# Classes by one comparison, keys read with a step, and the last layer's mask on ScalarE for four tiles at once

## The chip, the cores and the metric

The kernel runs on one core of one Trainium2 chip. A core has five engines with queues of their own: TensorE (PE in the profile, its weight loads PEld), VectorE (DVE), ScalarE (ACT), GpSimd (POOL) and SyncE (SP), which only starts DMAs. They work in parallel and wait for one another by semaphores; SBUF is the memory that all of them use, PSUM the one that TensorE writes its products to. The metric is the device time of one execution in microseconds. A kernel is timed in several runs, of which the median counts; one more execution is recorded by the hardware profiler.

## The reference, cut to what matters

The input is 16 graphs (batches) of 1024 nodes with 64 channels, and a dense, sparse-valued matrix `adj` of 1024 x 1024 for each. Layer 0 averages over neighbours; layer 1 takes quantiles over a thinned list of neighbours and passes them through two small matrix products:

```python
h = relu(layernorm(x))
x = x + (adj / clip(adj.sum(2), 1)) @ h           # layer 0
h = relu(layernorm(x))
# layer 1, for every node i of a graph:
nb      = (adj with ones on the diagonal, > 0), without i itself
m       = number of nb
skip    = (m + 1) // 2 if m > 10 and mask else 1
removed = every skip-th of nb, if skip > 1;  also removed from the other end
vals    = h[j] for all j still linked to i, i itself among them
agg     = 0.25*quantile(vals, .25) + 0.5*quantile(vals, .5) + 0.25*quantile(vals, .75)
y       = (relu((h + agg) @ W1 + b1) @ W2 + b2) * mask[i]
x       = x + y
```

The quantiles are taken per channel, so a node with m neighbours needs 64 columns of up to m + 1 values sorted. In these inputs an average node has few neighbours and a few nodes have very many.

## The kernel before, in words

**Tiles.** The 1024 nodes of a batch are 8 tiles of 128 rows. The batches are taken in four groups of four (`GROUPS`). Work on a batch is written as generators ("streams"), among them `loads`, `signs`, `transposes`, `products`, `channels`, `listing` and `endings`:

- `signs` and `listing` make, for each row of `adj`, the keys of its neighbours: ScalarE takes the sign (and sums it into `total`), VectorE multiplies by a falling column number (`sg<-sg,keyed`) and takes the eight largest of each of four segments (MAX8 into `rec`).
- `transposes` and `products` are layer 0: TensorE transposes `adj` into PSUM (`pt`), ScalarE copies to `att`, TensorE multiplies into `ps_small`, VectorE divides by the degree and adds `x` (`row<-ps_small,deg`).
- `channels` normalises and writes a table of rows (`tab`) to device memory.
- `endings` (line 772) sorts a batch's nodes by the length of their list. It makes a class number `d` for each node (lines 788 to 800) and from it `hot`, a one-hot array of 23 classes x 8 tiles. TensorE sums `hot` over nodes into a `ps_small` buffer `pc`; VectorE makes from it each node's place (`base`, `pos`, `to`); GpSimd scatters the rows to their places in `srt[g]`, one indirect DMA per tile.

When all four batches of a group have ended, `group(g)` (line 1294) reads back the sorted rows (`recs`), fetches one row of `adj` per partition for the nodes with most neighbours (`gat_rows<-in_adj_dram,hnodes_i`), corrects the table by a scatter (`tab<-drop,didx`), makes indices, and starts a `Job` (line 870) for each class of list length. The 32 nodes of each batch with the longest lists, 512 in all and four per partition, go to `long_lists` (line 1433), which takes them in four passes: each gathers one row of `adj` per partition (`gat_rows<-in_adj_dram,lnodes_i`) and makes the keys from it (`lkey`), since these lists are too long for `rec`.

**Jobs.** A group's sorted nodes are 31 tiles in ten length classes, of 1 to 6 tiles. A job gathers the lists from the table: one indirect DMA of GpSimd for each place of a list and tile (`places<-tab,idx`; `lplaces<-whole,lidx` for long lists). VectorE marks removed places (`rem`), sorts by a network of minima and maxima (`places`, `other`), and weighs the quantile places (`w`, `prod`). `layers` (line 1156) is the last step: for every chunk of up to four tiles TensorE sums and transposes the weighed rows (`pt`), ScalarE copies them (`ot`), TensorE multiplies by W1 (`ph`, a `ps_small` buffer), ScalarE applies the bias and the maximum (`hid`), TensorE multiplies by W2 (`py`, a `ps_small` buffer), and VectorE makes `y`, the masked product plus the residual. GpSimd scatters `y` to the output.

**What sets the order.** The tiles in PSUM come from small pools; `ps_small` has three buffers, shared by `products`, `endings`, `layers` and others. Each stream says at its yields on which engine it goes on and from when. A planner (`Plan`, line 246) keeps a modelled clock for every engine, and always runs the stream that can begin first, ties going by rank. The instructions are written to the engines' queues in that order, and for VectorE and GpSimd that order is kept (`manual_schedule`, line 377). So a due time is a position in a queue, not a wait. The constants that shift due times are `SLACK` (2.0), `LOOSE` (7.0) and `LATE` (14.0), in the planner's microseconds:

```python
yield "DVE", lambda: at(py) + LATE          # layers: y is due 14 after py
yield "PE", lambda: max(at(hid) + SLACK, room("ps_small", 3))
yield "POOL", lambda: at(y) + LATE          # the scatter of y
```

All instructions that the planner books pass through one helper at line 240, so the profile shows line 240 for nearly everything, and the groups are told apart by the names of their tiles.

Of the kernel before, what the change touches and what calls it, by code (L numbers as in the profile page):

```python
# [9 lines left out]
F32 = mybir.dt.float32  # L10
BF = mybir.dt.bfloat16
HF = mybir.dt.float16
I32 = mybir.dt.int32
U8 = mybir.dt.uint8
AF = mybir.ActivationFunctionType
OP = mybir.AluOpType
AX = mybir.AxisListType

P = 128
# [4 lines left out]
HUGE = 1.0e30  # L24
# [2 lines left out]

GROUPS = (4, 4, 4, 4)
NSEG = 4
STEPS = (16, 19, 22, 29, 39, 59, 79)  # L30
CLS = 15 + len(STEPS) + 1

# [10 lines left out]
LSEG = 8  # L45
# [181 lines left out]
SLACK = 2.0  # L227
LOOSE = 7.0
LATE = 14.0
# [16 lines left out]
class Plan:  # L246
# [33 lines left out]
    def at(self, *tiles):  # L280
        return max(self.ready.get(t.tensor.name, INF) for t in tiles)
# [104 lines left out]
def list_path(ctx, tc, x, adj, nodemask, w1, b1, w2, b2, out, go):  # L386
    nc = tc.nc
    B, N, C = x.shape
    H = w1.shape[1]
    CO = w2.shape[1]  # L390
    NT = N // P
# [15 lines left out]
    consts = ctx.enter_context(tc.tile_pool(name="consts", bufs=1))  # L407
    dram = ctx.enter_context(tc.tile_pool(name="dram", bufs=1, space=bass.MemoryType.DRAM))
    grp = ctx.enter_context(tc.tile_pool(name="grp", bufs=2))
# [22 lines left out]
    col_f = consts.tile([P, N], F32, name="col_f")  # L432
# [5 lines left out]
    nc.vector.memset(zero_f, 0.0)  # L438
    place1 = consts.tile([P, P], F32, name="place1")
    nc.vector.tensor_scalar(place1, col[:, :P], 1.0, None, op0=OP.add)  # L440
    cls_i = grp.tile([P, N], I32, name="gat_rows", bufs=1)[:, :CLS * NT]
    cls_i = cls_i.rearrange("p (c t) -> p c t", t=NT)
    nc.gpsimd.iota(cls_i, pattern=[[-1, CLS], [0, NT]], base=CLS - 1, channel_multiplier=0)
    cls = consts.tile([P, CLS, NT], F32, name="cls")
    nc.vector.tensor_copy(cls, cls_i)
    row_i = consts.tile([P, NT], I32, name="row_i")
    nc.gpsimd.iota(row_i, pattern=[[P, NT]], base=0, channel_multiplier=1)
    row_f = consts.tile([P, NT], F32, name="row_f")
# [323 lines left out]
    def endings(pool, now):  # L772

        first = lambda rank: rank - 3000
        for b, st in enumerate(batch):
            now[0] = b
            g = max(g for g in range(NG) if FIRST[g] <= b)
            size = GROUPS[g]
            yield "ACT", lambda: known(st, "rec", "row") if st["listed"] == NT else INF
            rec, total, row = st["rec"], st["total"], st["row"]  # L780

            for t in range(NT):
                nc.scalar.activation(
                    row[:, t, R0:R0 + 8 * NSEG], rec[:, t, :], AF.Relu, bias=before[:, t:t + 1]
                )


            yield "DVE", always
            found = new(pool, [P, NT, 8 * NSEG], BF, "found", 1)
            nc.vector.tensor_scalar(found, rec, 0.0, None, op0=OP.is_gt)  # L790
            d = new(tiny, [P, NT], F32, "d", 2)
            nc.vector.tensor_reduce(d, found, AX.X, OP.add)
            full = new(tiny, [P, NT], F32, "full", 2)
            nc.vector.tensor_reduce(
                full, found.rearrange("p t (s e) -> p t s e", e=8)[:, :, :, 7], AX.X, OP.max
            )
            nc.vector.scalar_tensor_tensor(d, full, float(STEPS[0]), d, op0=OP.mult, op1=OP.max)
            nc.vector.tensor_scalar(d, d, float(STEPS[0]), None, op0=OP.min)
            for s in STEPS[1:]:
                nc.vector.scalar_tensor_tensor(d, total, float(s), d, op0=OP.is_gt, op1=OP.add)  # L800
            free(rec)
            free(total)
            hot = new(tiny, [P, CLS, NT], BF, "hot", 2)
            nc.vector.tensor_tensor(
                hot, cls, d.unsqueeze(1).to_broadcast([P, CLS, NT]), OP.is_equal
            )
            yield "PE", lambda: max(at(hot), room("ps_small", 3))
            pc = new(ps_s, [P, HALF], F32, "ps_small", 3, users=1)
            K = CLS * NT
            flat = hot.rearrange("p c t -> p (c t)")  # L810
            nc.tensor.matmul(pc[:, :K], earlier, flat, start=True, stop=True)
            nc.tensor.matmul(pc[:, K:2 * K], ones, flat, start=True, stop=True)
            yield "DVE", lambda: at(pc) + SLACK
            base = new(tiny, [P, K], F32, "base", 2)
            nc.vector.memset(base[:, :1], 0.0)
            nc.vector.tensor_tensor_scan(
                base[:, 1:], pc[:, K:2 * K - 1], zeros[:, :K - 1], 0.0, op0=OP.add, op1=OP.add
            )
            nc.vector.tensor_tensor(base, base, pc[:, :K], OP.add)
            free(pc)  # L820
            nc.vector.tensor_tensor(base, base, flat, OP.mult)
            pos = new(tiny, [P, NT], F32, "pos", 2)
            nc.vector.tensor_reduce(pos, base.rearrange("p (c t) -> p t c", t=NT), AX.X, OP.add)
            low = new(tiny, [P, NT], I32, "low", 2)
            nc.vector.tensor_copy(low, pos)
            nc.vector.tensor_scalar(low, low, LSUB - 1, None, op0=OP.bitwise_and)
            if size == 2:
                aside = new(tiny, [P, 2, NT], F32, "aside", 2)
                for e, by in enumerate((-32.0, 64.0)):
                    nc.vector.tensor_scalar(  # L830
                        aside[:, e, :], pos, 64.0 / (e + 1), by, op0=OP.is_lt, op1=OP.mult
                    )
                for e in range(2):
                    nc.vector.tensor_tensor(pos, pos, aside[:, e, :], OP.add)
            nc.vector.tensor_scalar(
                pos, pos, float(size), float(LSUB * (b - FIRST[g])), op0=OP.mult, op1=OP.add
            )
            to = new(pool, [P, NT], I32, "to", 2)
            nc.vector.scalar_tensor_tensor(to, low, float(1 - size), pos, op0=OP.mult, op1=OP.add)
            if g == 0:  # L840
                plan.add(hubs(b, to), 10 * b + 8)
            for t in range(NT):
                yield "POOL", lambda: max(at(to), at(row)) + LOOSE if "normed" in st else INF, first
                scatter(srt[g], row[:, t, :], to[:, t:t + 1], sorts[g])
            free(row)
            progress["batches"] = b + 1
# [23 lines left out]
    class Job:  # L870
# [285 lines left out]
        def layers(self, terms, sources):  # L1156
# [17 lines left out]
            for t0 in range(0, T, 4):  # L1174
# [35 lines left out]
                        stop=(i == len(ts) - 1),  # L1210
                    )
                yield "DVE", lambda: at(py) + LATE
                for i, t in enumerate(ts):
                    nc.vector.scalar_tensor_tensor(
                        y[:, t, :], pv[:, i, :], self.mask[:, t:t + 1], x1[:, t, :],
                        op0=OP.mult, op1=OP.add,
                    )
                free(py)

            for t in range(T):  # L1220
                yield "POOL", lambda: at(y) + LATE
# [211 lines left out]
    def long_lists(pool):  # L1433

        yield "DVE", always
        rev = new(pool, [P, N], HF, "rev", 1)
        nc.vector.tensor_scalar(rev, col_f, -1.0, float(N), op0=OP.mult, op1=OP.add)
        yield "SP", always
        place = new(pool, [P, 1], I32, "lplace", 1)
        nc.vector.tensor_scalar(place, part, 7, None, op0=OP.bitwise_and)  # L1440
# [17 lines left out]
        for l in LORDER:  # L1458
# [17 lines left out]
            key = new(pool, [P, N], HF, "lkey", 1)  # L1476
            segs = key.rearrange("p (s q) -> p s q", s=LSEG)
            nc.vector.scalar_tensor_tensor(
                segs.rearrange("p s q -> p q s"), full.rearrange("p (q s) -> p q s", s=LSEG), 0.0,
                rev.rearrange("p (q s) -> p q s", s=LSEG), op0=OP.is_gt, op1=OP.mult,  # L1480
            )

            found = new(pool, [P, LSEG, max(LCAPS)], HF, "lfound", 1)
# [395 lines left out]
```

## Time and profile before

| | before |
|---|---|
| median of 3 runs | 1413.34 us (1410.7 to 1415.0) |
| profiled execution, its own time | 1414.18 us |
| span of the profile | 1412.4 us |
| TensorE (matmul) busy | 738.8 us, 52% |
| VectorE busy | 1228.7 us, 87% |
| ScalarE busy | 557.6 us, 39% |
| GpSimd busy | 963.8 us, 68% |
| mean granted TensorE clock | 0.71 of full |

The profiled execution took 1.8 us more than the span between its first and last recorded instruction. An engine's busy time leaves out what it spends on issuing, so GpSimd, nearly all of whose instructions are indirect DMAs, is fuller than its share: between two of them stands about 0.30 us that the profile calls issue. A group line gives line, engine, operation, output<-inputs, shapes and count, then busy us and mean ns of one, then the idle time of the engine just before the group and what ended it. A timeline line gives start and duration in us, and in brackets the idle time before and its releaser; consecutive like instructions stand on one line, with "xN".

The stages, by busy us in stretches of the span:

| stretch (us) | VectorE | ScalarE | GpSimd | what runs |
|---|---|---|---|---|
| 0 to 195 | 169.3 | 148.0 | 41.2 | batches of the first group |
| 195 to 860 | 577.8 | 372.6 | 510.3 | the other batches; gathers and sorts of groups 1 to 3 |
| 860 to 1250 | 346.1 | 19.5 | 300.8 | group 4's lists, long lists, sorting |
| 1250 to 1412 | 135.5 | 17.6 | 111.6 | last gathers, merges of long lists, last scatters |

### The profile page before, as it was taken

To read this page: it belongs to the slowest core of one execution; us is meant where nothing else is said; L and a number is where in the kernel's file an instruction comes from. 1 tells how busy PE (TensorE), PEld (TensorE's weight loads), DVE (VectorE), ACT (ScalarE), POOL (GpSimd) and SP (SyncE) were. 2 spreads that over 40 slices of the span, in tenths; PEclk is the share of its full clock that TensorE was granted. 3 is DMA by queue.
4 is the path that set the end of the run, shared out by engine and by line. 5 is a ranking of instruction groups with operands and counts; after the bars stand their busy time and mean duration, and the time that the engine had idled before them with its cause. 6 is when DMAs were issued, how large, how long until landed. Compare 5 with 4: busy or idle time off the path is not lost.

```text
span 1412.4 us, 14420 instructions
## 1 busy us (share of the span) xinstructions
PE 738.8 (52%) x3203; PEld 458.2 (32%) x3203; DVE 1228.7 (87%) x4150; ACT 557.6 (39%) x1603; POOL 963.8 (68%) x1115
## 2 busy tenths in 40 slices
PE   4878726376677657839856652002002232337685
PEld 2434413243443335425442331001001121226455
DVE  6999898999888898998999668886998899998985
ACT  6889763765554356865653520000000110001010
POOL 0042347777775787776778877775877777787764
PEclk9999868687787868968966865555555555557566
DMA  5464582443444245545541324211111111111110
GB/s 174 156 195 163 182 228 76 133 154 90 124 107 136 69 119 170 150 142 148 158 125 46 85 46 84 73 44 46 32 25 24 25 34 26 25 28 40 25 25 16
DMA packets 133834, 132.31 MB, mean 94 GB/s; under 512 B 99444, under 2 KB 102132, under 8 KB 133620
## 3 DMA queue, kind: packets, MB, share of 16 engines
q1 hardware_dynamic: 102220, 91.13, 21.8%
q0 software_dynamic: 31520, 40.19, 11.7%
q8 instruction: 27, 0.44, 0.1%
q14 instruction: 67, 0.55, 0.1%
HBM read 111.76 MB, written 23.61 MB: 96 GB/s over the span
## 4 chain that ended last, share of the span: by engine, by line
DVE 46%; POOL 18%; issue 10%; PE 10%; DMA 9%; ACT 6%; SPq 0%; DVEq 0%; POOLq 0%; ACTq 0%
POOL places L240 14%; DVE places L240 8%; DVE rec L240 6%; DVE other L240 5%; PE ps_small L240 5%; PE pt L240 5%; DVE lplaces L240 4%; DVE sg L240 2%; DMA at<-in_adj_dram 2%; DMA places<-tab,idx 2%; DVE l0other L240 2%; ACT sg L240 2%; POOL srt L240 2%; DVE prod L240 2%; DVE lkey L240 1%
## 5 line engine op out<-in xcount | busy, mean ns | idle before, releaser
L240 POOL DMA_INDIRECT places<-tab,idx x372 | 375.8, 1010 | 121.2 <-issue 104.2
L240 PE MATMUL pt<-ident,prod 128*128 128x128 f32 (+1 forms) x736 | 152.2, 367 | 385.8 <-DVE prod L240 330.9
L240 PE MATMUL ps_small<-att,h 128*65 128x512 f32 x512 | 261.7, 662 | 77.3 <-ACT h L240 55.9
L240 PEld LDWEIGHTS pt<-ident,prod 128*128 128x128 f32 (+1 forms) x736 | 126.0, 252 | 418.0 <-DVE prod L240 248.6
L240 POOL DMA_INDIRECT srt<-row,to x128 | 131.6, 1028 | 140.0 <-ACT row L240 118.9
L240 PE MATMUL pt<-ident,at 128*128 128x128 f32 x1024 | 164.0, 304 | 72.0 <-ACT att L240 52.7
L240 DVE MAX8 rec<-sg 128x8 f16<-128x256 f16 x512 | 180.2, 414 | 4.4
L240 ACT ACTIVATE sg<-at 128x1024 f16<-128x1024 f32 x128 | 134.8, 1054 | 102.0 <-DMA at<-in_adj_dram 65.6
L240 POOL DMA_INDIRECT lplaces<-whole,lidx x125 | 146.8, 1174 | 38.1 <-issue 36.9
L240 ACT COPY ot<-pt 128x128 f32<-128x128 f32 (+3 forms) x56 | 22.4, 400 | 377.4 <-PE pt L240 377.2
L240 PEld LDWEIGHTS pt<-ident,at 128*128 128x128 f32 x1024 | 125.7, 155 | 113.9 <-ACT att L240 77.6
L240 POOL DMA_INDIRECT places<-tab,last_idx x124 | 135.0, 1089 | 37.8 <-issue 35.0
L240 ACT COPY att<-pt 128x512 f32<-128x512 f32 x256 | 140.7, 584 | 26.8 <-PE pt L240 25.3
L240 PEld LDWEIGHTS ps_small<-att,h 128*65 128x65 f32 x512 | 76.1, 155 | 220.9 <-issue 125.0
L240 POOL DMA_INDIRECT out_dram<-y,nodes_i x93 | 95.7, 1029 | 20.6 <-issue 12.7
L240 DVE TENSOR_TENSOR sg<-sg,keyed 128x1024 f16<-128x1024 f16 x128 | 87.4, 682 | 15.6 <-ACT sg L240 15.6
L240 ACT ACTIVATE wu<-wu 128x39 f32<-128x39 f32 (+9 forms) x40 | 9.4, 235 | 152.0 <-DVE wu L240 152.0
L240 PE MATMUL ps_small<-ot,w_sb 128*128 128x128 f32 (+3 forms) x112 | 52.0, 554 | 30.8 <-DVE base L240 11.9
L240 DVE TENSOR_TENSOR places<-places,other 128x128 f32<-128x128 f32 (+6 forms) x160 | 56.4, 355 | 3.4
L240 PE MATMUL ps_small<-w_sb,hid 128*128 128x64 f32 x256 | 50.1, 332 | 1.9 <-ACT hid L240 1.6
L240 DVE TENSOR_TENSOR places<-other,places 128x128 f32<-128x128 f32 (+5 forms) x136 | 48.8, 366 | 1.7
L240 DVE TENSOR_TENSOR other<-places 128x256 f32<-128x256 f32 (+4 forms) x124 | 48.1, 388 | 1.9
(292 smaller groups left out, 1600.7 us busy)
## 6 DMA issues: line engine op xcount, KB each, us to landing
at<-in_adj_dram SPq DMA_DIRECT2D x64, 1024.0 KB, 5.6
places<-tab,idx POOLq DMA_INDIRECT x372
whole<-tab SPq DMA_DIRECT2D x4, 1057.0 KB
tab<-row SPq DMA_DIRECT2D x16, 264.0 KB, 3.8
xt<-in_x_dram SPq DMA_DIRECT2D x16, 256.0 KB, 6.7
S<-srt SPq DMA_DIRECT2D x12, 192.0 KB, 2.6
y<-srt SPq DMA_DIRECT2D x12, 192.0 KB, 2.7
srt<-row,to POOLq DMA_INDIRECT x128
```

What stands on the lines that cost most here:

```text
L240: ins = getattr(self._engine, op)(*args, **kwargs)
```

## The change

Three places change, all within `list_path`.

*Classes.* `STEPS` holds all limits of the list length, 1 to 16 as well as 19 to 79, and the number of classes stays 23. In `endings` the count of found keys is no longer made: `total`, the sum of signs that ScalarE left, is raised to 17 where a segment's eighth key is positive, and compared with all limits at once (`above`, 24 x 8 per partition); the difference of neighbouring limits' answers is `hot`. The array of class numbers `cls`, made by an iota of GpSimd and a copy of VectorE at the start, gives way to `limits`, made by 24 memsets of VectorE.

*Last step of `layers`.* For chunks of three or four tiles (in these inputs 20 chunks, all of four), ScalarE multiplies each tile's product by the mask, in place in PSUM, due `SLACK` after `py` but behind the yield with `LATE` that was there before; a further yield with `LATE` follows, and one VectorE instruction adds the residual for the whole chunk. Chunks of one or two tiles keep their instructions, with the yield of `LATE` twice in a row.

*Keys of long lists.* `rev` is laid out in the order of the segments when it is made, once. The key instruction then writes its output in a row and reads the gathered row with a step of `LSEG` (8) elements; before, it read in a row and wrote with a step.

```diff
--- before.py
+++ after.py
@@ -27,8 +27,8 @@
 
 GROUPS = (4, 4, 4, 4)
 NSEG = 4
-STEPS = (16, 19, 22, 29, 39, 59, 79)
-CLS = 15 + len(STEPS) + 1
+STEPS = (*range(1, 17), 19, 22, 29, 39, 59, 79)
+CLS = len(STEPS) + 1
 
 
 
@@ -438,11 +438,9 @@
     nc.vector.memset(zero_f, 0.0)
     place1 = consts.tile([P, P], F32, name="place1")
     nc.vector.tensor_scalar(place1, col[:, :P], 1.0, None, op0=OP.add)
-    cls_i = grp.tile([P, N], I32, name="gat_rows", bufs=1)[:, :CLS * NT]
-    cls_i = cls_i.rearrange("p (c t) -> p c t", t=NT)
-    nc.gpsimd.iota(cls_i, pattern=[[-1, CLS], [0, NT]], base=CLS - 1, channel_multiplier=0)
-    cls = consts.tile([P, CLS, NT], F32, name="cls")
-    nc.vector.tensor_copy(cls, cls_i)
+    limits = consts.tile([P, CLS + 1, NT], F32, name="limits")
+    for c, limit in enumerate((HUGE, *reversed(STEPS), -HUGE)):
+        nc.vector.memset(limits[:, c, :], float(limit))
     row_i = consts.tile([P, NT], I32, name="row_i")
     nc.gpsimd.iota(row_i, pattern=[[P, NT]], base=0, channel_multiplier=1)
     row_f = consts.tile([P, NT], F32, name="row_f")
@@ -786,24 +784,20 @@
 
 
             yield "DVE", always
-            found = new(pool, [P, NT, 8 * NSEG], BF, "found", 1)
-            nc.vector.tensor_scalar(found, rec, 0.0, None, op0=OP.is_gt)
-            d = new(tiny, [P, NT], F32, "d", 2)
-            nc.vector.tensor_reduce(d, found, AX.X, OP.add)
             full = new(tiny, [P, NT], F32, "full", 2)
             nc.vector.tensor_reduce(
-                full, found.rearrange("p t (s e) -> p t s e", e=8)[:, :, :, 7], AX.X, OP.max
-            )
-            nc.vector.scalar_tensor_tensor(d, full, float(STEPS[0]), d, op0=OP.mult, op1=OP.max)
-            nc.vector.tensor_scalar(d, d, float(STEPS[0]), None, op0=OP.min)
-            for s in STEPS[1:]:
-                nc.vector.scalar_tensor_tensor(d, total, float(s), d, op0=OP.is_gt, op1=OP.add)
+                full, rec.rearrange("p t (s e) -> p t s e", e=8)[:, :, :, 7], AX.X, OP.max
+            )
+            nc.vector.tensor_scalar(full, full, 0.0, 17.0, op0=OP.is_gt, op1=OP.mult)
+            nc.vector.tensor_tensor(total, total, full, OP.max)
             free(rec)
+            above = new(tiny, [P, CLS + 1, NT], BF, "above", 1)
+            nc.vector.tensor_tensor(
+                above, total.unsqueeze(1).to_broadcast([P, CLS + 1, NT]), limits, OP.is_gt
+            )
             free(total)
             hot = new(tiny, [P, CLS, NT], BF, "hot", 2)
-            nc.vector.tensor_tensor(
-                hot, cls, d.unsqueeze(1).to_broadcast([P, CLS, NT]), OP.is_equal
-            )
+            nc.vector.tensor_tensor(hot, above[:, 1:, :], above[:, :CLS, :], OP.subtract)
             yield "PE", lambda: max(at(hot), room("ps_small", 3))
             pc = new(ps_s, [P, HALF], F32, "ps_small", 3, users=1)
             K = CLS * NT
@@ -1210,12 +1204,24 @@
                         stop=(i == len(ts) - 1),
                     )
                 yield "DVE", lambda: at(py) + LATE
-                for i, t in enumerate(ts):
-                    nc.vector.scalar_tensor_tensor(
-                        y[:, t, :], pv[:, i, :], self.mask[:, t:t + 1], x1[:, t, :],
-                        op0=OP.mult, op1=OP.add,
+                if len(ts) > 2:
+                    yield "ACT", lambda: at(py) + SLACK
+                    for i, t in enumerate(ts):
+                        nc.scalar.mul(pv[:, i, :], pv[:, i, :], self.mask[:, t:t + 1])
+                    yield "DVE", lambda: at(py) + LATE
+                    some = slice(t0, t0 + len(ts))
+                    nc.vector.tensor_tensor(
+                        y[:, some, :], pv[:, :len(ts), :], x1[:, some, :], OP.add
                     )
-                free(py)
+                    free(py)
+                else:
+                    yield "DVE", lambda: at(py) + LATE
+                    for i, t in enumerate(ts):
+                        nc.vector.scalar_tensor_tensor(
+                            y[:, t, :], pv[:, i, :], self.mask[:, t:t + 1], x1[:, t, :],
+                            op0=OP.mult, op1=OP.add,
+                        )
+                    free(py)
 
             for t in range(T):
                 yield "POOL", lambda: at(y) + LATE
@@ -1434,7 +1440,10 @@
 
         yield "DVE", always
         rev = new(pool, [P, N], HF, "rev", 1)
-        nc.vector.tensor_scalar(rev, col_f, -1.0, float(N), op0=OP.mult, op1=OP.add)
+        nc.vector.tensor_scalar(
+            rev.rearrange("p (s q) -> p s q", s=LSEG),
+            col_f.rearrange("p (q s) -> p s q", s=LSEG), -1.0, float(N), op0=OP.mult, op1=OP.add,
+        )
         yield "SP", always
         place = new(pool, [P, 1], I32, "lplace", 1)
         nc.vector.tensor_scalar(place, part, 7, None, op0=OP.bitwise_and)
@@ -1476,8 +1485,8 @@
             key = new(pool, [P, N], HF, "lkey", 1)
             segs = key.rearrange("p (s q) -> p s q", s=LSEG)
             nc.vector.scalar_tensor_tensor(
-                segs.rearrange("p s q -> p q s"), full.rearrange("p (q s) -> p q s", s=LSEG), 0.0,
-                rev.rearrange("p (q s) -> p q s", s=LSEG), op0=OP.is_gt, op1=OP.mult,
+                segs, full.rearrange("p (q s) -> p s q", s=LSEG), 0.0,
+                rev.rearrange("p (s q) -> p s q", s=LSEG), op0=OP.is_gt, op1=OP.mult,
             )
 
             found = new(pool, [P, LSEG, max(LCAPS)], HF, "lfound", 1)
```

## The prediction

> **What bounds the kernel now.** I read the page's first part and its 40 slices (row DVE and row POOL, 35.3 us to a digit), then the groups by shape, then the waits of VectorE and of GpSimd, then the timeline where the two meet. First the page:
>
> ```profile
> PE 738.8 (52%) x3203; PEld 458.2 (32%) x3203; DVE 1228.7 (87%) x4150; ACT 557.6 (39%) x1603; POOL 963.8 (68%) x1115
> DVE  6999898999888898998999668886998899998985
> POOL 0042347777775787776778877775877777787764
> L240 POOL DMA_INDIRECT places<-tab,idx x372 | 375.8, 1010 | 121.2 <-issue 104.2
> ```
>
> VectorE is busy 87% and has no long hole. GpSimd reads as 68%, but from the first gather of a list place (194.8 us) it is as full: an indirect DMA occupies it about 1.0 us and 0.30 us of issue follow, so its real pitch is 1.25 to 1.35 us. The idle spans on it that are longer than an issue add up to only 33 us between 195 and 1376. So two engines run nearly full side by side from 195 us on, and either alone would hold the end close to where it is. The waits name what each still loses:
>
> ```profile
> DVE y L240 <- PE ps_small L240: 31.6, 4, 12.0
> DVE rem L240 <- DMA places<-tab,idx: 19.9, 5, 7.7
> POOL tab L240 <- DVE base L240: 10.0, 1, 10.0
> POOL gat_rows L240 <- DVE lnodes_i L240: 9.3, 1, 9.3
> ```
>
> (us in total, times, longest.) VectorE waits for TensorE in four `y`, and for gathers; GpSimd waits for VectorE. The timeline ties two of these together, and shows a third loss:
>
> ```profile
> 892.78 3.94 POOL L240 DMA_INDIRECT places<-tab,idx  x1 [0.30 <-issue]
> 891.69 4.70 DVE L240 SCALAR_TENSOR_TENSOR lkey<-gat_rows,rev 128x1024 f16<-128x1024 f32 x1
> 953.80 1.23 DVE L240 TENSOR_TENSOR prod<-other,w 128x1024 f32<-128x1024 f32 x1
> 966.51 0.86 DVE L240 SCALAR_TENSOR_TENSOR y<-ps_small,recs,y 128x64 f32<-128x64 f32 x4 [11.48 <-PE ps_small L240]
> 985.43 1.01 POOL L240 DMA_INDIRECT gat_rows<-in_adj_dram,lnodes_i  x1 [9.30 <-DVE lnodes_i L240]
> ```
>
> At 953.80 VectorE makes a chunk's products and then stands at that chunk's `y` until 966.5 (a second one, at 1100.6, stands 11.97). That lateness reaches `lnodes_i`, for which GpSimd idles 9.3 us. And each of the four 4.70 us key steps holds an indirect DMA of GpSimd for 3.94 us, where a free one takes 0.94: 4 x 3.0 = 12 us.
>
> **What the skill says.** The Trainium skill, "SBUF — State Buffer", section "SBUF: two separate sides", calls the port pair that VectorE and GpSimd share an exclusive lock; an operation on one blocks the other, and descriptors of GpSimd's DMAs starve meanwhile. The 3.94 beside the 4.70 agrees. "ScalarE: Activation LUTs", section "What ACT_TABLE_LOAD costs": an ACTIVATE with one pointer operand takes about 280 + 0.833 N ns, 333 for 64 elements; this trace has 335 for `ln_sq` 128x64 with one such operand.
>
> **The change, part by part.** Durations are from these groups (busy us, mean ns):
>
> ```profile
> L240 DVE SCALAR_TENSOR_TENSOR d<-total,d 128x8 f32<-128x8 f32 x96 | 16.0, 167 | 3.3
> L240 DVE TENSOR_REDUCE d<-found 128x8 f32<-128x256 bf16 x16 | 6.7, 420 | 0.5
> L240 DVE TENSOR_TENSOR hot<-cls,d 128x184 bf16<-128x184 f32 x16 | 5.6, 352 | 0.5
> L240 DVE SCALAR_TENSOR_TENSOR y<-ps_small,recs,y 128x64 f32<-128x64 f32 x93 | 21.0, 275 | 23.5 <-PE ps_small L240 23.5
> L240 DVE SCALAR_TENSOR_TENSOR lkey<-gat_rows,rev 128x1024 f16<-128x1024 f32 x4 | 18.8, 4700 | 0.1
> L240 DVE TENSOR_TENSOR row<-ps_small,deg 128x256 f32<-128x256 f32 x32 | 13.6, 425 | 1.1
> ```
>
> *Classes, 16 batches.* Today `found` to `hot` of one batch runs from 175.69 to 178.40: 2.71 us. Removed: `found` 225, the reduction 420, the two `d` 169 and 243, six steps of 167, `hot` 352. The short reduction (0.20) stays. Added: a TENSOR_SCALAR and a TENSOR_TENSOR of 8 elements (0.17 to 0.24 each), the comparison over 192 (352 for 184 today, so 0.36), the difference over 184 bf16. The last is not in the trace: "VectorE: DVE Perf Modes", section "The perf-mode tier table", gives bf16 TENSOR_TENSOR twice the rate, so 0.25 by estimate, 0.35 if not. Sum 1.2, saving 1.5 us a batch: **24 us** (22 to 25). At the start an iota on GpSimd and a copy go, and 24 memsets of about 0.06, 1.4 us, come; VectorE's 8.3 us wait for `marks` covers them, and uncovered they cost just that.
>
> *Last layer, 20 chunks of four tiles* (80 of 124 tiles). Four `y` take 0.86 us in the timeline; one TENSOR_TENSOR from PSUM over 256 takes 0.43. Saving 20 x 0.43 = **9 us** (13 by means, which overlap). ScalarE gets 80 x 0.33 = 27 us; it is 39% busy, and from 860 to 1250 us nearly idle (19 us of 390), so this hides; on a chunk's own chain it puts four masks, some 1.4 us. The mask is a new wait of ScalarE for TensorE: behind it in the queue stand `sg` (for which VectorE's sign keys wait) and the `att` copies (for which TensorE's transposes wait). It is emitted behind the old yield, so 14 after `py` on the planner's clock, and I take no wait; if TensorE runs late, the bound is the last matmuls of a chunk, 1.6 us, 20 times. The single tile whose `y` ends the run (1405.09, waiting 7.67) is not touched.
>
> *The same part moves `y`.* A second LATE, 14.0 on the planner's clock, stands ahead of it, so the planner sets `y` at least 28 after the last matmul instead of 14, and VectorE's order is the planner's. In the built order of before, 0.2 and 2.6 us of VectorE work lie between the two stalled chunks' products and their `y`, while the chain (7.2 of transposes, 0.58, 1.13, 0.69, 1.6) needs 11.5. In the changed order the least of the third group's chunks has 15. Both stalls should go: **23.4 us** of idle. The price is queued elsewhere: `py` holds one of three `ps_small` buffers longer, and the next tile that wants it is TensorE's (messages, class counts), which VectorE and then GpSimd's scatters read. Counting in the built orders, cases with under 9 us of VectorE work between a `py` release and the reader of the next tile in that buffer go from 9 to 18. Price of each: between 0 and 4 us (GpSimd's waits at 436 and 648 for VectorE are 4 and 6). I take 0, because in that stage GpSimd still has gathers ahead in its queue when a row comes late; without that cover 9 more cases would cost 36 us.
>
> *Long lists, 4 keys.* The write becomes contiguous and one input is read with a 32-byte step. Bounds: 1.28 (the same operation contiguous, `gat_rows<-col_f,lS,gat_rows`) and 4.70. The skill's SBUF page, section "Door 1: The DMA port swizzle", says that each access to a new 16-byte line pays. Nearest row: `pos<-base` reads 184 elements with that step in 484 ns, against 512 contiguous in 665 (`ln_s`); less a fixed 0.15 that is 1.8 ns an element, against 1.0. So I take 2.0: 4 x 2.7 = **11 us** of VectorE, and the lock shrinks with it: 4 x 2.5 = **10 us** of GpSimd. `rev`'s step costs at most a microsecond, once.
>
> Direct saving on VectorE: 24 + 9 + 11 = 44 us of 1228.7, and 23 of idle.
>
> **Where it goes.** GpSimd must not be overtaken. I follow its landmarks, with the VectorE work that the changed order puts ahead of each. First gather 194.8 -> about 191 (two batches' classes less, one transposed tile moved ahead). `tab<-drop` 430.4 -> about 413: VectorE leads, 21 us less work. Third group's `gat_rows`, 648.0: GpSimd is back to back and this chain scatter-rows-gather has its own latency, so it stays near 648, but 8 more indirect DMAs lie ahead of it. Fourth, 865.1 -> 863, 5 more ahead. Last `gat_rows<-in_adj_dram,lnodes_i` 985.4 -> 967: the 9.3 us wait goes, three key stalls of 2.5 with it, and the first `y` stall. From there VectorE needed 427 us; less the second stall 12, `y` 5.5 and the fourth key 2.7, that is 407: 1374. GpSimd after its last gather (1343.5, now about 1305) needs the 69 us tail as before: 1374 too. Span 1373.5; the profiled run lay 1.8 outside its span (1414.2 against 1412.4) and 0.8 above the median, so I forecast **1374 us** in the timed runs, 39 below 1413.3.
>
> **Rivals.**
> *GpSimd keeps the end (18 in 100).* The stalls move to `rem` (19.9 already, waiting for gathers) and new idle takes back half. For: the same 893 indirect DMAs, at 1.3 us. Against: 8 more are issued early. Gain: key stalls 10 and first gather and readiness about 8: 1395.
> *All of VectorE's work pays (17).* 44 + 23, less 4 where GpSimd sits: 1350. For: 87%. Against: GpSimd alone, its waits gone, ends near 1355.
> *The key stays at 4.7 (10).* Stepped reads as dear as stepped writes; 11 and 10 come off the sum, partly overlapping: 1388.
> *Slower (9).* In the batch stage (195 to 860) 11 or so long-list chunks run. A `py` kept 14 longer can starve `ps_small`: TensorE waits, rows come late, GpSimd's scatters wait behind in its fixed order. At 4 us of new GpSimd idle per chunk that is 44: the gain of 39 is gone, and 1418. Against: GpSimd's queue holds gathers enough there, so that a late `row` costs nothing until it reaches the head. It decides if over 3.5 us a chunk are lost.
>
> **How the numbers follow.** The forecast has 46 in 100, with a spread of about 12. The five cases: 1350 (17), 1374 (46), 1388 (10), 1395 (18), 1418 (9). Leaving one in ten at each end gives 1350 to 1403. A measurement tells 0.3%, 4 us. Faster: the first four less the upper tail of the rival at 1395, 0.88; same 0.03; slower 0.09.
>
> **What would show it.** Right: VectorE's busy time near 1185; `d` and `found` gone, a class block of 1.2 us; `y` for four tiles at 0.43 with no wait of 11 us at it; `lkey` near 2.0 and no 3.94 beside it; ScalarE up 27. GpSimd's busy time some 10 lower, last gather near 1305. Wrong: new waits of `ps_small` readers (`row`, `base`, `y`) in the batch stage, a later first gather, or a `rem` sum that grows by what `y` lost.

## The result, and the profile after

The changed kernel takes 1434.53 us (median of 4 runs, 1431.74 to 1438.46) against 1413.46 of the kernel before (4 runs beside them): a ratio of 1.0145, with a 95% interval of 1.0125 to 1.0165. It is slower by 21 us where 39 us less were forecast. The profiled execution took 1431.74 us, with a span of 1430.0.

The page of the kernel after, first part and the rows of VectorE and GpSimd in 40 slices (35.75 us to a digit):

```profile
PE 742.2 (52%) x3203; PEld 466.1 (33%) x3203; DVE 1190.7 (83%) x4001; ACT 576.9 (40%) x1683; POOL 947.9 (66%) x1121
DVE  6987897999669778967777796688899989999996
POOL 0043247777745784777678577877787777778765
```

VectorE lost 38 us of work and the kernel got 18 us longer. Compare VectorE's row with that of before: the middle, slices 11 to 24, is where most 8s and 9s became 6s and 7s.

The groups by shape (busy us, mean ns), which answer to those that the costs were taken from:

```profile
L240 DVE TENSOR_TENSOR above<-total,limits 128x192 bf16<-128x192 f32 x16 | 5.7, 358 | 0.5
L240 DVE TENSOR_TENSOR hot<-above 128x184 bf16<-128x184 bf16 x16 | 4.1, 254 | 0.6
L240 DVE TENSOR_TENSOR y<-ps_small,y 128x256 f32<-128x256 f32 x20 | 8.3, 415 | 0.0
L240 DVE SCALAR_TENSOR_TENSOR lkey<-gat_rows,rev 128x1024 f16<-128x1024 f32 x4 | 8.0, 1993 | 0.1
L240 ACT ACTIVATE ps_small<-ps_small,recs 128x64 f32<-128x64 f32 x60 | 17.4, 290 | 16.2 <-PE ps_small L240 15.3
```

Each operation of VectorE costs what was put down for it, and a mask of ScalarE costs less (290 ns instead of 335), so the loss is not in them. The waits of VectorE and of GpSimd (us in total, times, longest):

```profile
DVE sg L240 <- ACT sg L240: 58.5, 9, 14.7
DVE rem L240 <- DMA places<-tab,idx: 15.5, 3, 6.7
DVE base L240 <- PE ps_small L240: 12.9, 5, 6.0
DVE deg L240 <- PE ps_small L240: 11.4, 2, 7.0
...
DVE y L240 <- PE ps_small L240: 6.9, 1, 6.9
```

```profile
POOL gat_rows L240 <- DVE gbasep L240: 19.5, 2, 16.5
...
POOL places L240 <- DVE rem L240: 14.5, 1, 14.5
POOL srt L240 <- ACT hid L240: 12.8, 2, 12.6
```

The waits at `y` went from 31.6 to 6.9 us, as forecast. In their place VectorE waits 58.5 us for ScalarE's signs, where the kernel before had

```profile
DVE sg L240 <- ACT sg L240: 15.6, 5, 7.3
```

It is the batches that are late: GpSimd then waits at the head of its queue for a gather's indices, for a free list, for a row. Its timeline has the three largest waits after its first gather, all in the batch stage:

```profile
423.36 0.95 POOL L240 DMA_INDIRECT gat_rows<-in_adj_dram,hnodes_i  x1 [16.54 <-DVE gbasep L240]
...
562.19 0.94 POOL L240 DMA_INDIRECT places<-tab,idx  x1 [14.47 <-DVE rem L240]
...
808.94 0.99 POOL L240 DMA_INDIRECT srt<-row,to  x1 [12.62 <-ACT hid L240]
```

One sum places the loss. From the first gather of a list place to the fourth group's `gat_rows` GpSimd issues n indirect DMAs; the stretch is n times a pitch (the mean time from one to the next), plus its idle spans longer than 0.6 us (from its timeline), which the pitch leaves out:

| kernel | first gather | n | pitch | idle | fourth `gat_rows` | from there to the end |
|---|---|---|---|---|---|---|
| before | 194.8 | 495 | 1.308 | 23.0 | 865.1 | 547.3 |
| after | 197.9 | 500 | 1.304 | 65.5 | 915.6 | 514.4 |

At 865 us the changed kernel is 50 us behind: 3 from the start, 5 DMAs more (6.5), and 42.5 of new idle, less 2 of pitch. After that it gains 33 us, about what the prediction expected of that part. So the question is one of the batch stage: are the queues' new waits due to the new instructions (above all the masks in ScalarE's queue), or to the order in which the planner now puts all the work?

### The profile page after: what moved, and what is told of

Its sections match the earlier page's. It is cut to its first block, busy times and chain, and to the rows that moved or that the text cites. A ratio compares the mean times of both kernels' runs of the same rounds, so it can differ in the third digit from the quotient of the medians.

```text
span 1430.0 us, 14333 instructions
## 1 busy us (share of the span) xinstructions
PE 742.2 (52%) x3203; PEld 466.1 (33%) x3203; DVE 1190.7 (83%) x4001; ACT 576.9 (40%) x1683; POOL 947.9 (66%) x1121
## 3 DMA queue, kind: packets, MB, share of 16 engines
q1 hardware_dynamic: 102220, 91.13, 21.7%
q0 software_dynamic: 31520, 40.19, 12.8%
## 4 chain that ended last, share of the span: by engine, by line
DVE 32%; POOL 24%; PE 12%; issue 12%; DMA 11%; ACT 8%; SPq 0%; DVEq 0%; POOLq 0%; ACTq 0%
POOL places L240 13%; PE ps_small L240 7%; DVE places L240 6%; POOL lplaces L240 6%; PE pt L240 5%; DMA at<-in_adj_dram 4%; DVE other L240 4%; DVE rec L240 4%; POOL out_dram L240 3%; ACT sg L240 2%; DMA places<-tab,idx 2%; DVE sg L240 2%; ACT att L240 2%; DMA places<-tab,last_idx 1%; DMA gat_rows<-in_adj_dram,hnodes_i 1%
## 5 line engine op out<-in xcount | busy, mean ns | idle before, releaser
L240 PE MATMUL pt<-ident,prod 128*128 128x128 f32 (+1 forms) x736 | 163.6, 387 | 416.7 <-DVE prod L240 364.2
L240 PEld LDWEIGHTS pt<-ident,prod 128*128 128x128 f32 (+1 forms) x736 | 133.4, 267 | 449.1 <-DVE prod L240 222.5
L240 PE MATMUL ps_small<-att,h 128*65 128x512 f32 x512 | 250.2, 638 | 29.1 <-ACT h L240 11.6
L240 PE MATMUL pt<-ident,at 128*128 128x128 f32 x1024 | 174.0, 315 | 89.1 <-ACT att L240 52.9
L240 PEld LDWEIGHTS pt<-ident,at 128*128 128x128 f32 x1024 | 133.4, 161 | 136.7 <-ACT att L240 80.6
L240 POOL DMA_INDIRECT lplaces<-whole,lidx x125 | 134.9, 1079 | 38.1 <-issue 37.5
L240 DVE TENSOR_TENSOR sg<-sg,keyed 128x1024 f16<-128x1024 f16 x128 | 87.3, 682 | 58.5 <-ACT sg L240 58.5
L240 PE MATMUL ps_small<-ot,w_sb 128*128 128x128 f32 (+3 forms) x112 | 50.8, 545 | 42.9 <-ACT ot L240 26.5
L240 ACT ACTIVATE row<-row,ln_s,ln_v 128x64 f32<-128x64 f32 x128 | 44.3, 430 | 16.1 <-DVE ln_s L240 16.1
```

Of the source, the lines that this page charges most:

```text
L240: ins = getattr(self._engine, op)(*args, **kwargs)
```

## The experiments

Two theories stood against each other. *Parts*: one part's instructions do the harm, most likely the mask's. *Order*: what the planner books for the new instructions and due times gives other queues, and those are worse, whatever is in them. A product buffer that is held longer, because `y` comes later, belongs to the second: it follows from the place of `y` in the queue, and no run separates the buffer from the place.

### Each part alone, and the change without the mask

`keys_only`, `classes_only` and `mask_only` are the kernel before with that one part of the diff; `no_mask` is the changed kernel with this put back:

```diff
                 yield "DVE", lambda: at(py) + LATE
-                if len(ts) > 2:
-                    yield "ACT", lambda: at(py) + SLACK
-                    for i, t in enumerate(ts):
-                        nc.scalar.mul(pv[:, i, :], pv[:, i, :], self.mask[:, t:t + 1])
-                    yield "DVE", lambda: at(py) + LATE
...
+                for i, t in enumerate(ts):
+                    nc.vector.scalar_tensor_tensor(
+                        y[:, t, :], pv[:, i, :], self.mask[:, t:t + 1], x1[:, t, :],
+                        op0=OP.mult, op1=OP.add,
                     )
```

> The kernel before with the new keys alone. They come after the batch stage, and the planner books the same cost for them, so both theories expect the order of before and a gain: 2.7 us of VectorE in each of four keys (1.99 instead of 4.70 after the change) and 2 to 3 us of GpSimd in each: 1400 to 1405.

> The kernel before with the new classes alone. Theory A (the last layer's part alone does the harm: a kept product buffer and a new wait in ScalarE's queue make the batch stage late): the classes save their 24 us of VectorE work and some 10 to 25 us of time, so 1390 to 1403, and the wait of VectorE for signs stays near the 16 us of before. Theory B (every change of what the planner books reshuffles the queues, and the reshuffled order of the batch stage is the worse one): no gain or a loss here too, 1410 to 1440, with waits of 8 us and more of VectorE for signs as after the change.

> The kernel before with the new last step of the layers alone (mask on ScalarE in PSUM, one addition for four tiles, the due time of y twice as late). Theory A: this alone is slower than before, 1430 to 1455, more than the whole change is, because the gains of the other two parts are missing. Theory B: it is no worse than the other parts; the stalls of 11.5 and 12.0 us at y go and it ends at 1385 to 1410.

> The changed kernel with the last step of the layers put back (classes and keys stay). Theory A: the two gains without the harm, 1380 to 1395. Theory B: 1400 to 1435, near the changed kernel.

| run | ratio to before | 95% interval | median us |
|---|---|---|---|
| keys_only | 0.9898 | 0.9873 to 0.9924 | 1401.68 |
| classes_only | 1.0057 | 1.0043 to 1.0071 | 1423.15 |
| mask_only | 1.0094 | 1.0065 to 1.0123 | 1427.60 |
| no_mask | 0.9981 | 0.9967 to 0.9995 | 1411.89 |

The keys gain 1.0%, as both theories expected. Theory *parts* in its first form falls: the classes, which only take work away, lose on their own. `mask_only` at 1427.6 fits neither theory's range (1430 to 1455, or 1385 to 1410), and `no_mask` at 1411.9 lies in that of *order*. The three single ratios add up to 0.5% slower, where the whole change is 1.45% slower: the parts don't simply add.

Where the keys' gain comes from is seen in the timeline of `keys_only`:

```profile
895.77 1.99 DVE L240 SCALAR_TENSOR_TENSOR lkey<-gat_rows,rev 128x1024 f16<-128x1024 f32 x1
896.98 1.55 POOL L240 DMA_INDIRECT places<-tab,idx  x1 [0.30 <-issue]
```

4.70 became 1.99 on VectorE, and the indirect DMA beside it 1.55 to 1.67 instead of 3.94: 11 us of VectorE and 9 of GpSimd, in a part of the run in which both are nearly full, gave 13 us.

### The order held, and the order alone

The planner keeps VectorE's and GpSimd's order by what it books. So a part's new instructions can be issued past it, with the old ones booked in their place: the two queues are then, instruction for instruction, those of the kernel before except for what is replaced. `classes_kept` does this with the classes:

```diff
+            raw = tc.nc.vector
...
+            raw.tensor_scalar(full, full, 0.0, 17.0, op0=OP.is_gt, op1=OP.mult)
+            raw.tensor_tensor(total, total, full, OP.max)
...
+            book("tensor_scalar", found_b, rec)
+            book("tensor_reduce", d_b, found_b)
+            book("tensor_reduce", full, found_b[:, :, :NSEG])
...
```

(`raw` issues without booking, `book` books without issuing.)

`mask_kept` does it with the last layer: the masks follow a yield for ScalarE, `y` is due 14 after `py` and booked as four instructions. `all_kept` has both, and the keys. `mask_order` is the reverse, the instructions of before in the queues of `mask_only` (the cut is against `mask_only`):

```diff
-                        nc.scalar.mul(pv[:, i, :], pv[:, i, :], self.mask[:, t:t + 1])
+                        plan.note(
+                            "ACT", "mul", (pv[:, i, :], pv[:, i, :], self.mask[:, t:t + 1]), {}
+                        )
                     yield "DVE", lambda: at(py) + LATE
                     some = slice(t0, t0 + len(ts))
-                    nc.vector.tensor_tensor(
-                        y[:, some, :], pv[:, :len(ts), :], x1[:, some, :], OP.add
-                    )
+                    for i, t in enumerate(ts):
+                        tc.nc.vector.scalar_tensor_tensor(
+                            y[:, t, :], pv[:, i, :], self.mask[:, t:t + 1], x1[:, t, :],
+                            op0=OP.mult, op1=OP.add,
+                        )
+                    plan.note("DVE", "tensor_tensor", (y[:, some, :], pv[:, :len(ts), :], x1[:, some, :]), {})
```

By the starts in the traces, GpSimd's order in `classes_kept` and `all_kept` is that of before except for the iota that went, and VectorE's except for what is replaced and about a dozen neighbours. What this doesn't hold is the order of TensorE and ScalarE, which a second scheduler sets after the planner: in `classes_kept_4` about 250 of TensorE's 3203 recorded matmuls and 150 of ScalarE's 1603 instructions stand elsewhere than before. `mask_order_4` and `mask_only` differ in fewer places, about 30 and 16.

> The new classes alone, but booked with the planner at the costs of the old ones, so that the order of VectorE and of GpSimd is instruction for instruction that of the kernel before, apart from the replaced ones. Work theory (the new instructions themselves are no gain, or a wait of theirs takes it back): 1418 to 1428, as classes_only. Order theory (classes_only lost by its reshuffled queues): faster than before by 8 to 24 us, 1390 to 1406, and the wait of VectorE for signs back near 16 us.

> The mask on ScalarE and the one addition alone, with y booked as before and due 14 after its product, so that VectorE and GpSimd keep the order of before. Order theory: about before or a little faster, 1402 to 1416; the two stalls at y stay and grow by the masks' 1.2 to 2 us each. Mask theory (the wait in ScalarE's queue does the harm): 1424 or more, with waits of VectorE for ln_v of ScalarE as in mask_only (32 us).

> The instructions of before, four per chunk on VectorE and none on ScalarE, in the order of VectorE and GpSimd that mask_only has (y late, the product buffer kept as long). Order theory: slower than before, 1420 to 1435, like mask_only. Mask theory: near before or faster, 1395 to 1415, since the two stalls at y are gone and ScalarE's queue has nothing new in it.

> All three parts of the change in the order of VectorE and GpSimd that the kernel before has. Order theory: the sum of the gains without the reshuffling, keys 13, classes 8 to 24, mask 0 to 10: 1370 to 1392. Work theories: 1420 to 1435, as the change itself.

In this set of runs the kernel before itself took 1795 us, and in two repeats 1814 and 1817. The waits of TensorE in `classes_kept` show a difference:

```profile
PE pt L240 <- issue: 222.2, 45, 26.5
PE ps_small L240 <- issue: 111.5, 30, 17.4
```

TensorE stands up to 26.5 us for nothing that the profile shows, 334 us in these two rows; where the kernel before takes 1413 us, neither it nor any of its variants has such a row. The mean granted clock is lower too, 0.66 or 0.67 instead of 0.71 to 0.72. Which of these is cause and which effect is not shown. VectorE is busy 67% of the span there, so work saved on it counts for little, and what these runs can show is harm.

> The kernel of classes_kept once more: on the chip of that run the kernel before took 1795 us[...], so the parts could not be told apart there. Where the kernel before takes its 1413 us: work theory 1418 to 1428, as classes_only; order theory 1390 to 1406.

> The kernel of mask_kept once more, for the same reason. Order theory: 1402 to 1416. Mask theory (the wait in ScalarE's queue does the harm): 1424 or more.

> The kernel of mask_order once more, for the same reason. Order theory: 1420 to 1435, like mask_only. Mask theory: 1395 to 1415.

> The kernel of all_kept once more, for the same reason. Order theory: the sum of the gains without the reshuffling, 1370 to 1392. Work theories: 1420 to 1435, as the change itself.

> The kernel of all_kept on a third chip; on the two before, the kernel before took 1795 and 1814 us, and this one tied with it (1.0035 and 1.0002). Where the kernel before takes its 1413 us: order theory 1370 to 1392, since VectorE is the fuller engine there and its saved work counts; work theories 1420 to 1435.

> The kernel of mask_order on a third chip; on the two before it lost 1.8 and 2.2% though it runs the instructions of before. Order theory: 1420 to 1440 here. Mask theory: 1395 to 1415.

> The kernel of classes_kept on a third chip; on the two before it tied (0.9995 and 1.0000). Order theory: 1390 to 1406, since here VectorE's 24 us less count in the batch stage. Work theory, or a batch stage that VectorE doesn't bound at all: 1410 to 1428.

| kernel | before at 1795 us | before at 1814 us | before at 1817 us |
|---|---|---|---|
| classes_kept | 0.9995 (0.9965 to 1.0026) | 1.0000 (0.9975 to 1.0025) | 0.9993 (0.9965 to 1.0021) |
| mask_kept | 1.0049 (1.0022 to 1.0076) | 0.9994 (0.9968 to 1.0020) | |
| all_kept | 1.0035 (1.0004 to 1.0066) | 1.0002 (0.9982 to 1.0023) | 0.9962 (0.9934 to 0.9990) |
| mask_order | 1.0177 (1.0103 to 1.0252) | 1.0222 (1.0172 to 1.0272) | 1.0237 (1.0155 to 1.0318) |

Each time the new instructions in the old order stay within half a per cent of before, and each time the old instructions in the new order lose about two per cent. In the last runs the kernel before took its usual time, 1412 to 1413 us; `mask_kept` has no run there:

> The kernel of all_kept once more. Three chips[...] (the kernel before took 1795 to 1817 us) gave 1.0035, 1.0002 and 0.9962. Where the kernel before takes its 1413 us: order theory 1370 to 1392; work theories 1420 to 1435. Where it takes about 1800 again: 1790 to 1825, a tie.

> The instructions of before in the order of mask_only, on a chip of the usual pace if it falls on one (the last call did: all three parts in the order of before gave 0.9921 there). If the order alone does the harm: 1424 to 1436, as mask_only or a little more. If the masks in ScalarE's queue do: 1400 to 1416.[...]

> The new classes in the order of before, on a chip of the usual pace if it falls on one. If saved work on VectorE counts in the batch stage: 1390 to 1402. If that stage is paced by TensorE's and ScalarE's queues, so that VectorE only waits more for signs: 1406 to 1414, and the wait for signs is longer than before's 16 us.[...]

| run | instructions | order | ratio | 95% interval | median us |
|---|---|---|---|---|---|
| classes_only | classes new | new | 1.0057 | 1.0043 to 1.0071 | 1423.15 |
| classes_kept_4 | classes new | before | 0.9991 | 0.9980 to 1.0001 | 1411.36 |
| mask_only | mask new | new | 1.0094 | 1.0065 to 1.0123 | 1427.60 |
| mask_order_4 | all as before | that of mask_only | 1.0112 | 1.0090 to 1.0135 | 1427.39 |
| after | all new | new | 1.0145 | 1.0125 to 1.0165 | 1434.53 |
| all_kept_4 | all new | before | 0.9921 | 0.9897 to 0.9945 | 1399.96 |

**The order does the harm.** `mask_order_4` has no mask on ScalarE; its VectorE, ScalarE and TensorE run as many instructions as before (4150, 1603 and 3203), and its GpSimd four memsets of 0.12 us more. It takes what `mask_only` takes. `all_kept_4` has every operation of the change and is 0.8% faster than before; between it and the change lie 2.2 points. All three pairs point the same way. In the classes' pair no due time of `y` changes, so there it is the order alone; in the mask's pair the order includes the later `y` and the buffer that it holds.

**And in the order of before, the classes' saved work is worth nothing in the batch stage.** The order theory expected 1390 to 1406 of `classes_kept` and 1370 to 1392 of `all_kept`; they give 1411 and 1400, the classes a tie and the whole no better than the keys alone. VectorE's busy time in stretches from about the first gather to about the fourth group's `gat_rows` (the view by windows; columns: the stretch and its length, then the busy time and count of TensorE, its weight loads, VectorE, ScalarE and GpSimd), first of before, then of `classes_kept_4`, then of `mask_order_4`, then of after:

```profile
195.00:866.00 671.00, 423.92 (x1784) 246.88 (x1785) 583.40 (x1921) 372.61 (x1136) 514.02 (x628) 0.77 0.42 117
```

```profile
193.00:861.00 668.00, 423.94 (x1780) 245.49 (x1781) 567.84 (x1841) 371.75 (x1136) 512.51 (x628) 0.77 0.42 118
```

```profile
192.00:887.00 695.00, 431.23 (x1814) 257.78 (x1814) 584.30 (x1922) 373.88 (x1138) 515.61 (x631) 0.77 0.40 113
```

```profile
198.00:916.00 718.00, 428.14 (x1824) 258.74 (x1821) 563.97 (x1812) 379.52 (x1173) 518.75 (x638) 0.75 0.40 110
```

In `classes_kept_4` VectorE works 15.6 us less than before, and the stretch from the first gather to the fourth group's `gat_rows` is 2 us shorter. GpSimd's sum says why: 495 DMAs at 1.307 and 20.9 of idle, against 495 at 1.308 and 23.0. It is nearly full, its order and count are the same, so it sets the length; VectorE's idle spans over 0.6 us grow from 54 to 69 us, and its wait for signs from 15.6 to 24.5. The expectation that came true had named TensorE's and ScalarE's queues as the pace of that stage; the sum points to GpSimd's.

In `mask_order_4` the same sum has 498 DMAs at 1.306 and 45.0 of idle: 22 us more than before with VectorE's work unchanged, 3.9 more for the three DMAs that its order puts ahead, and a start 3.2 earlier. It is 21.7 us late at the fourth group's `gat_rows` and makes good 10 of them afterwards.

The classes' order loses by another path. In `classes_only` the first gather is at 199.9, 5.1 us late, and 493 DMAs follow at 1.319 with 26.6 of idle: 11.5 us late at the fourth group's `gat_rows`, of which only 3.6 are new idle and 5.4 are pitch. `keys_only`, in the order of before, has a pitch of 1.314, so part of that can be the execution's.

**What a wait of the new order looks like.** The largest of VectorE in the batch stage of `mask_order_4`, from its timelines:

```profile
474.52 0.36 SPq L240 DMA_DIRECT2D y<-srt  x1
474.99 1.02 SPq L240 DMA_DIRECT2D at<-in_adj_dram  x2
...
480.45 1.06 ACT L240 ACTIVATE sg<-at 128x1024 f16<-128x1024 f32 x1 [14.07 <-DMA at<-in_adj_dram]
...
483.02 0.20 DVE L240 RECIPROCAL ln_v<-ln_v 128x8 f32<-128x8 f32 x1 [14.89 <-ACT ln_v L240]
```

SyncE issues DMAs in order. At its head stands `y<-srt`, the residual rows of a later job, which need one of the six `y` buffers, and that is free only when an older `y` has been scattered; its waits in the window 470 to 476 are 11.1 us for such scatters. Behind it stand two loads of `adj`. When the scatter has landed, all go out at once; ScalarE has stood 14 us at the sign of those rows, with `ln_v` and a `hid` behind it in its own queue, and so VectorE stands 14.9 us at `ln_v` and TensorE 12.1 at the product of `hid`.

Such a hold is not new. The kernel before has one whose `y<-srt` goes out at 482.4 us, and ScalarE waits longer there, but VectorE less:

```profile
491.60 1.06 ACT L240 ACTIVATE sg<-at 128x1024 f16<-128x1024 f32 x1 [15.77 <-DMA at<-in_adj_dram]
...
494.93 0.20 DVE L240 RECIPROCAL ln_v<-ln_v 128x8 f32<-128x8 f32 x1 [5.84 <-ACT ln_v L240]
```

In that order VectorE still had sorting and weighing to do, to 489.1 us, before it came to `ln_v`; in `mask_order_4` it comes there at 468.1 and stands. The sums don't tell a bad order from a good one either. Counting ScalarE's waits over 0.6 us for loads of `adj` that went out in a burst (issues less than 0.6 us apart) beginning with `y<-srt` or `recs<-srt` gives 35 us before, 48 in `classes_only`, 39 in `mask_order_4` and 50 in after, but also 43 in `classes_kept_4` and 42 in `all_kept_4`, which lose nothing. So longer holds of SyncE's queue are not shown to be the cause.

What GpSimd loses in `mask_order_4` stands for the most part at three scatters of rows:

```profile
509.48 0.98 POOL L240 DMA_INDIRECT srt<-row,to  x1 [8.63 <-ACT row L240]
...
547.42 0.99 POOL L240 DMA_INDIRECT srt<-row,to  x1 [8.40 <-ACT row L240]
...
590.04 0.99 POOL L240 DMA_INDIRECT srt<-row,to  x1 [7.46 <-issue]
```

They make 24.5 of its 45.0 us of idle; before, no scatter of rows waits more than 0.73 us in that stretch. Of the three large waits of the changed kernel, the 16.5 us at the second group's `gat_rows` is in the classes' order too (18.3 in `classes_only`, 17.7 in `no_mask`), while the other two come with the parts together: in no kernel with one part alone does a gather of a list place wait over 7.2 us in that stretch, or a scatter of rows over 8.5. Which link of the chains between the queues makes each of these late is open: no run took one away, and a kernel with more `y` buffers, or with the loads of `adj` on another queue, was not tried.

## Why the prediction was wrong, point by point

- **The prices.** Right. Class block 1.2 us forecast, 1.18 by the group means; the addition for four tiles 0.43, measured 0.415; `lkey` 2.0, measured 1.99; the DMA beside it from 3.94 to 1.67. (The section of the Trainium skill that the prediction names for this, in "SBUF — State Buffer", tells of starved descriptors for VectorE's 2-port modes; for an operation with two inputs, as here, it is these two measured times that show it.) VectorE's busy time 1185 forecast, 1190.7 measured. ScalarE rose by 19 instead of 27 us: a mask in PSUM takes 290 ns, less than the 333 of the formula and the 335 of `ln_sq`, and four in a row take 1.25 us.
- **The stalls at `y`.** Right in the changed kernel: 31.6 us of waits became 6.9. In `all_kept_4`, where `y` keeps its old place, they are there, 12.8 and 15.6 us long where 11.5 and 12.0 stood. But the second LATE alone doesn't remove both: in `mask_only` one of 14.6 us stays.
- **The part after the fourth group's `gat_rows`.** Right in length: 1373.5 less 863 is 510.5 us forecast, 514.4 measured, 33 less than before. In part this is luck: each part alone shortens it by 10.7 (keys), 9.8 (mask) and 0.7 us (classes), together 21, and the rest comes with an order that the prediction didn't work out. Its tail of 69 us was also misread: the last gather of the kernel before starts at 1360.5, not at 1343.5, so "last gather near 1305" had a wrong base; it is at 1370.9 after.
- **The landmarks up to there.** Wrong, and this is nearly the whole miss. First gather 191 forecast, 197.9 measured; `tab<-drop` 413, measured 438.2; third group's `gat_rows` 648, measured 683.5; fourth 863, measured 915.6. The span was missed by 56.5 us, and 52.6 of it are there by then. The counts of DMAs ahead, 8 and 5 more, were right.
- **The step that failed** is the price of the reordering. For the mask's part it was put at 0: "because in that stage GpSimd still has gathers ahead in its queue when a row comes late". For the classes' part no such price stands beside the 24 us, though a cheaper booking moves the queues as well. GpSimd had 23.0 us of idle in that stretch before, 45.0 with the mask's order alone (`mask_order_4`) and 65.5 after: its queue is in order too, and a scatter or a gather came to its head before what it waits for was ready. The bound that the text put beside it, 36 us without the cover, is near the 42.5 of new idle, but it counted late tiles of `ps_small` in the mask's part, and the largest wait, 16.5 us, comes with the classes' order, so the nearness is luck.
- **The second error, of kind.** Landmarks were moved by the VectorE work ahead of them. `classes_kept_4` shows that in the batch stage this work is not the measure: taking 15.6 us away with the order held shortened it by 2. The first gather's and the `tab<-drop` landmarks rested on that, and the 24 us of the classes were counted for a stage that GpSimd's count and pitch set. That the same prediction called GpSimd as full as VectorE from 195 us on should have been a warning.
- **The rivals.** The one that ended slower gave 1418, by 44 us of new GpSimd idle: the amount is near (42.5), the mechanism named, a starved `ps_small`, isn't shown. For it speak VectorE's waits for TensorE's `ps_small` at `base` (2.0 before, 12.9 after) and at `deg` (11.4 after), which the prediction named as a sign of being wrong; against it that these are 1.4 and none in `mask_order_4`, which holds `py` as long and is slower than before all the same. TensorE's waits for a `y` (16.6 us before, 21.5 there, 12.2 after) don't follow the loss. The rival in which GpSimd keeps the end and the stalls move to `rem` didn't happen: `rem` waits 15.5 us for gathers instead of 19.9. The 1400 of `all_kept_4` is near its 1395, but there the stalls at `y` are still in place.

## What to carry to other kernels

Where a planner or a scheduler places the work, a change of costs or due times is a change of every queue. Price the order first: for the fullest in-order queue, count its instructions, its pitch and its idle spans in the stage, and ask which of them the change moves. Work saved on another engine bought nothing in that stage here. To tell the two apart, issue the new instructions with the old bookings, and the old instructions with the new ones. And before calling a wait new, look for it in the kernel before: here a hold of one kind cost VectorE 5.8 us in one order and 14.9 in the other, by what it still had to do meanwhile.

## What the runs showed of the hardware

A SCALAR_TENSOR_TENSOR over 1024 fp32 took 1.28 us with everything contiguous (`gat_rows<-col_f,lS,gat_rows`, output fp32), 1.99 with one input read with a step of 32 bytes, and 4.70 with its half-precision output written with a step of 256 bytes; an indirect DMA of GpSimd, 0.94 us when free, took up to 1.67 beside the second and 3.94 beside the third. The kernel before had medians of 1412 to 1414 us in some sets of runs and of 1795 to 1817 in others. The record gives one and the same chip number to a set of each kind (1817 us, and half an hour later 1412), so it isn't shown that the chip makes the difference. In the long ones TensorE stands for nothing that the profile shows, and a difference in VectorE's work that shows at 1413 us can vanish there.
